# Who issues the stores of ScalarE's products: SyncE's queue or ScalarE's own

## The chip, the cores and the metric

The kernel runs on one core of a Trainium2 chip. The metric is the device time of one execution in microseconds (us). Below, the engines carry the names of the profile: PE is TensorE, with PEld its weight loads; DVE is VectorE, ACT is ScalarE, POOL is GpSimd, and SP is SyncE. Each engine works through its own list of instructions in order, and semaphores tie the lists together. A DMA is an instruction on the list of the engine that issues it; the bytes are then moved by 16 DMA engines beside the others. A trailing q, as in SPq or ACTq, means the engine's sequencer, which issues and waits.

## The reference

Two layers over a batch of 8 images of 384 channels and 32 x 32 pixels, all in float32. Cut to what matters:

```python
# layer 0, for each image: L = 1024 pixels as a sequence, forward and reversed
xn = rmsnorm(x)
u, z = split(xn @ in_proj)
u = silu(causal_conv1d(u) + b)
dt, B, C = split(u @ x_proj)                   # 24 + 16 + 16 columns
delta = softplus(dt @ dt_proj + dt_b)
h[t] = exp(delta * A) * h[t-1] + (delta * u) * B     # 16 states per channel
y = (sum_n h * C + u * D) * silu(z)
g = (y_forward + y_reversed) @ out_proj * scale_mod
x = x + res_scale * (g + sigmoid(dwconv3x3(xn)) * xn)
# layer 1
t = x + attention(layernorm(x))                # 6 heads of 64, causal, 1024 tokens
out = t + gelu(layernorm(t) @ kron(a, b).T) @ kron(c, d).T
```

## The kernel before

**An order planned ahead.** The whole program, 8 images through both layers, is first written as a list of operations, each with an engine, a cost, the values it reads and writes, and a wished-for time `at`. `Plan.run` (line 170) then plays the engines and one DMA pipe with these costs and fixes one order for everything. DMAs stand in that plan as operations of "SP" with a cost of 0.6 us. The loop at lines 1451 to 1461 emits the instructions in the planned order; each engine gets its own in that order.

**Stages of one image.** `project` makes u before the convolution, and `gates` makes z, both through `into` (line 707): PE multiplies, ACT copies each half out of PSUM (line 725), and for u the tile `ut` is stored to the DRAM array `urd` (line 727). `gates` then takes silu of the three tiles `zt` on ACT (line 740) and stores each in two halves to `uzd` through `blocks` (line 648, with `which` 1 for z and 0 for u). `prepare` loads `ct<-urd`, convolves, takes silu on ACT, and calls `products` (line 851), which makes B, C and dt in a tile `xd`; rows of B and C are stored to `bcd` (line 865). `deltas` sums the u of both directions on POOL (tile `us`, stored by `blocks` with `which` 0) and calls `delta` (line 868), which makes delta (`de`, stored to `ded` from POOL's result) and delta times u on POOL. The latter is split into three bf16 parts: ACT casts a part (line 905), two DMAs store its halves to `dusd` (line 907), POOL subtracts the part from the remainder (line 913), and so on. The tiles `part` share two buffers.

**The scan.** `scans` and `group` run the recurrence in 96 steps an image, on tiles `dA` of 128 rows (16 states by 8 channels) and 1024 time steps: a DMA loads delta (`dA<-ded`, 512 KB, 12 buffers), ACT takes exp (line 994), PE spreads the parts of delta u (`du<-dusd`) into PSUM tiles `b`, DVE multiplies by B (line 1009) and scans (line 1017), POOL multiplies by C (line 1020), PE sums over the states into `y`. `local`, `finish`, `attention`, `mix` and `forward` are the rest; while one image is scanned, the stages before the scan of the next images and those behind the scan of the same image run between its steps.

**What orders the DMAs.** All 1998 DMAs are issued by SP. The framework that turns the list into a program gives each DMA one of eight completion semaphores (DMAHW0 to DMAHW7) in turn, and each DMA first waits until the one that had this semaphore before, eight DMAs earlier in the program, has landed. So at most eight are on their way at a time. Buffers in SBUF and arrays in DRAM add waits of their own.

Of the kernel before, what the change touches and what calls it, by code (L numbers as in the profile page):

```python
# [17 lines left out]
P = 128  # L18
B, C, H, W = 8, 384, 32, 32
L = H * W  # L20
CT = C // P
# [3 lines left out]
NS = 16  # L25
# [15 lines left out]
KI, KO = 32, 12  # L41
# [63 lines left out]
class Plan:  # L105
# [13 lines left out]
    def op(self, engine, cost, fn, reads=(), writes=(), at=None, table=None, nbytes=0, holds=()):  # L119


        o = Op()
        o.engine, o.cost, o.fn, o.table, o.nbytes = engine, cost, fn, table, nbytes
        o.at = self.at if at is None else at
        o.placed = o.urgent = at is not None
        o.vals, o.allocs, o.users, o.ready, o.done = [], [], [], 0.0, None
        deps = set()

        def meets(a, b):
            return a is None or b is None or a == b  # L130

        for v in reads:
            v, part = v if isinstance(v, tuple) else (v, None)
            deps.update(w for w, q in v.writes if meets(part, q))
            v.reads.append((o, part))
            o.vals.append(v)
        for v in writes:
            v, part = v if isinstance(v, tuple) else (v, None)
            deps.update(w for w, q in v.writes if meets(part, q))
            deps.update(r for r, q in v.reads if meets(part, q))  # L140
            if part is None:
                v.writes, v.reads = [], []
            if v.kind is not None and v.left == 0 and v not in o.allocs:
                o.allocs.append(v)
            v.writes.append((o, part))
            o.vals.append(v)
        for v in holds:
            if v.left == 0 and v not in o.allocs:
                o.allocs.append(v)
            o.vals.append(v)  # L150
        deps.discard(o)
        o.vals = list(dict.fromkeys(o.vals))

        o.after, slot_of = [], set()
        for v in o.vals:
            v.left += 1
            if v in o.allocs:
                v.first = o
            elif v.first is not None and v.first not in deps:
                slot_of.add(v.first)  # L160
        for d in slot_of:
            d.after.append(o)
        o.waits = len(deps) + len(slot_of)
        for d in deps:
            d.users.append(o)
        o.index = len(self.ops)
        self.ops.append(o)
        return o
# [119 lines left out]
def conv_attn_hybrid_kernel(  # L288
# [20 lines left out]
    nc = tc.nc  # L309
# [28 lines left out]
    def half(hf):  # L338
        return slice(hf * HALF, (hf + 1) * HALF)
# [4 lines left out]
    def grid(t):  # L344
        return t.rearrange("p (r w) -> p r w", w=W)
# [63 lines left out]
    plan = Plan({k: n for k, (n, _) in kinds.items()})  # L409
    op = plan.op  # L410

    def dma(dst, src, reads, writes, nbytes, **kw):

        op("SP", 0.6, lambda: nc.sync.dma_start(dst(), src()), reads, writes, nbytes=nbytes, **kw)

    def tl(name, shape=(P, L), dtype=F32):
        return Val("t", list(shape), name, dtype)

    def bank(name):
        return Val("psm", [P, HALF], name)  # L420

    def accumulate(terms, p, cost, holds=(), **kw):

        for i, (args, reads) in enumerate(terms):
            first, last = i == 0, i == len(terms) - 1

            def term(args=args, first=first, last=last):
                mm(*args(), first, last)

            op("PE", cost, term, reads, [p], holds=holds if first else (), **kw)  # L430
# [39 lines left out]
    def arrays(shape, name, n, dtype=F32):  # L470
        return [array(shape, f"{name}_{i}", dtype) for i in range(n)]
# [10 lines left out]
    bcd = [arrays([2 * NS, L], f"bcd{d}", 2) for d in range(2)]  # L482
# [165 lines left out]
    def blocks(i, which, m, t, part):  # L648

        for a in range(2):  # L650
            dma(
                lambda a=a: uzd[i][2 * m + a].t[which].rearrange("(h p) t -> p h t", p=HC),
                lambda a=a: t.t[a * HC : (a + 1) * HC, :], [t], [(uzd[i][2 * m + a], part)], HC * L * 4,
            )

    def in_weights(b, w):
# [50 lines left out]
    def into(b, w, xp, win):  # L707

        s = b % 2
        ts = []  # L710
        for m in range(CT):
            t = tl(f"{'uz'[w]}t_{b}_{m}")
            for hf in range(NH):
                p = bank(f"pi_{b}_{w}_{m}_{hf}")

                accumulate(
                    [
                        (
                            lambda p=p, m=m, hf=hf, c=c: (grid(p.t), win.t[:, c, chans(m)], inside(xp[c].t, hf)),
                            [(xp[c], hf), win],  # L720
                        )
                        for c in range(CT)
                    ], p, pe(HALF), [t],
                )
                op("ACT", act(HALF), lambda p=p, t=t, hf=hf: nc.scalar.copy(t.t[:, half(hf)], p.t), [p], [(t, hf)])
            if w == 0:
                dma(
                    lambda m=m: urd[s].t[chans(m), TAPS - 1 : TAPS - 1 + L], lambda t=t: t.t, [t], [(urd[s], m)],
                    P * L * 4,
                )  # L730
            ts.append(t)
        return ts
# [118 lines left out]
    def products(b, d, us, wc):  # L851

        s = b % 2
        xd = tl(f"xd_{b}_{d}")
        for hf in range(NH):
            p = bank(f"px_{b}_{d}_{hf}")

            accumulate(
                [
                    (lambda p=p, hf=hf, c=c: (p.t, wc.t[:, c, 0:P], us[d][c].t[:, half(hf)]), [us[d][c], wc])  # L860
                    for c in range(CT)
                ], p, pe(HALF), [xd],
            )
            op("ACT", act(HALF), lambda p=p, hf=hf: nc.scalar.copy(xd.t[:, half(hf)], p.t), [p], [(xd, hf)])
        dma(lambda: bcd[d][s].t, lambda: xd.t[CT * KI : P, :], [xd], [bcd[d][s]], 2 * NS * L * 4)
        return xd

    def delta(b, d, c, du, xd):

        s = b % 2  # L870
        n = f"{b}_{d}_{c}"


        e, de, ln, w = (tl(f"{q}_{n}") for q in ("e", "de", "ln", "w"))
        ps = [bank(f"pd_{n}_{hf}") for hf in range(NH)]

        def both():
            for hf in range(NH):
                r = slice((c + hf) % CT * KI, (c + hf) % CT * KI + RANK)
                mm(ps[hf].t, w_dt[hf].t[r, :], xd.t[r, half(hf)])  # L880

        op("PE", pair(HALF), both, [xd] + [(w, c) for w in w_dt], ps, holds=[e, de])
        for hf in range(NH):

            def split(p=ps[hf], hf=hf):
                nc.scalar.activation(e.t[:, half(hf)], p.t, AF.Abs, bias=col("dt_b", c))
                nc.scalar.activation(de.t[:, half(hf)], p.t, AF.Relu, bias=col("dt_b", c))  # L887

            op("ACT", 2 * act(HALF) + 0.1, split, [ps[hf]], [(e, hf), (de, hf)])

        def logs():
            nc.scalar.activation(e.t, e.t, AF.Exp, scale=-1.0)
            nc.scalar.activation(w.t, e.t, AF.Identity, bias=ones[:, 0:1])
            nc.scalar.activation(ln.t, w.t, AF.Ln)
            nc.scalar.activation(w.t, w.t, AF.Identity, bias=minus)

        op("ACT", 4 * act(L) + 0.2, logs, [], [e, ln, w], table=EXP)
        op("POOL", pool(L), lambda: nc.gpsimd.tensor_sub(w.t, e.t, w.t), [e], [w])
        op("POOL", pool(L), lambda: nc.gpsimd.tensor_add(de.t, de.t, ln.t), [ln], [de])
        op("POOL", pool(L), lambda: nc.gpsimd.tensor_add(de.t, de.t, w.t), [w], [de])  # L900
        dma(lambda: ded[d][s].t[chans(c)], lambda: de.t, [de], [(ded[d][s], c)], P * L * 4)
        op("POOL", pool(L), lambda: nc.gpsimd.tensor_mul(du.t, de.t, du.t), [de], [du])
        for k in range(3):
            part = Val("t2", [P, L], f"part_{n}_{k}", BF16)
            op("ACT", act(L), lambda part=part: nc.scalar.copy(part.t, du.t), [du], [part])  # L905
            for hf in range(NH):
                dma(
                    lambda k=k, hf=hf: dusd[d][s].t[c * RG : (c + 1) * RG, hf, k],
                    lambda part=part, hf=hf: part.t[:, half(hf)], [part], [(dusd[d][s], (c, k, hf))], P * HALF * 2,
                )  # L910
            if k < 2:
                op(
                    "POOL", pool(L), lambda part=part: nc.gpsimd.tensor_sub(du.t, du.t, part.t), [part], [du]  # L913
                )
# [609 lines left out]
```

## Time and profile before

| | |
|---|---|
| three runs | 3931.32, 3935.32 and 3963.04 us, median 3935.32 |
| the profiled execution | 3941.6 us |
| its span, from the first to the last instruction | 3939.9 us |
| busy share of the span | PE 90%, DVE 85%, POOL 76%, ACT 72% |
| DMA packets' time on the one data queue, as a share of 16 engines' span | 77.5% |
| mean granted TensorE clock | 0.929 |

Busy shares are means over stages with different limits. The page also has each engine's share in 40 slices of the span, the chain of work that ended last, and the costliest groups of instructions by line; answers of the trace give waits, single lines, stretches and the order of time.

### The profile page before, as it was taken

The page shows a single profiled execution, that of the slowest core. Times are in us where ns is not written, and L with a number is a line of the kernel's source. Part 1 is how long each engine was busy: PE and PEld are TensorE (multiplying, and loading weights), DVE is VectorE, ACT ScalarE, POOL GpSimd, SP SyncE. Part 2 cuts the span into 40 slices and gives each one's busy share as a digit, 9 for nine tenths or more (in the row PEclk, how much of TensorE's full clock was granted, in tenths as well). Part 3 has the DMA queues.
Part 4 walks back from the last instruction along what each step waited for, and adds up shares of the span by engine and source line. Part 5 has one row for each costly group of instructions (what it writes and reads, how often), then busy time and mean ns, then how long its engine had stood idle before and what let it go on. Part 6 is the DMA issues. An engine that isn't in the chain of part 4 may idle for free.

```text
span 3939.9 us, 54075 instructions
## 1 busy us (share of the span) xinstructions
PE 3545.6 (90%) x17970; PEld 1386.8 (35%) x17970; DVE 3362.0 (85%) x4403; ACT 2821.3 (72%) x4465; POOL 2999.4 (76%) x2370
## 2 busy tenths in 40 slices
PE   7477768899999999899999999999999988999998
PEld 3011112443244432443234432443234431443363
DVE  1489998899988999899998999799898999999522
ACT  4665645887788867786788868887778866676464
POOL 2888986997699956998589966998579966676231
PEclk9587778999999999899999999999998998999999
DMA  8889899689966998689966998779976897678101
GB/s 266 238 253 281 250 262 245 179 235 269 273 201 201 259 264 244 183 241 256 276 207 187 255 271 249 199 230 248 257 231 170 219 253 189 168 197 227 44 9 37
DMA packets 301999, 858.92 MB, mean 218 GB/s; under 512 B 38312, under 2 KB 91576, under 8 KB 301720
## 3 DMA queue, kind: packets, MB, share of 16 engines
q1 hardware_dynamic: 301720, 855.47, 77.5%
q8 instruction: 143, 2.34, 0.3%
q14 instruction: 136, 1.11, 0.1%
HBM read 696.44 MB, written 160.68 MB: 218 GB/s over the span
## 4 chain that ended last, share of the span: by engine, by line
DVE 33%; PE 25%; DMA 15%; POOL 12%; issue 7%; ACT 7%; SPq 1%; POOLq 0%; DVEq 0%; ACTq 0%
DVE dA L1017 20%; DVE b L1009 7%; DMA dA<-ded 5%; POOL dA L1020 5%; PE t L1254 3%; PE pc L331 3%; PE y L331 2%; PE s L331 2%; PE pq L331 2%; POOL p L1244 2%; PE b L331 2%; DVE mx L1190 2%; DMA dusd<-part 1%; DMA yg<-ygd 1%; PE pi L331 1%
## 5 line engine op out<-in xcount | busy, mean ns | idle before, releaser
L1020 POOL TENSOR_TENSOR dA<-dA,bc 128x1024 f32<-128x1024 f32 x768 | 1808.7, 2366 | 579.5 <-DVE dA L1017 405.8
L1017 DVE TENSOR_TENSOR_SCAN dA<-dA,b 128x512 f32<-128x512 f32 x1536 | 1906.1, 1242 | 36.4 <-ACT dA L994 18.1
L1009 DVE TENSOR_TENSOR b<-b,bc 128x512 f32<-128x512 f32 x1536 | 986.3, 683 | 166.7 <-PE b L331 160.6
L994 ACT ACTIVATE dA<-dA,nA 128x1024 f32<-128x1024 f32 x768 | 864.3, 1146 | 311.6 <-DMA dA<-ded 270.6
L331 PE MATMUL b<-du,dup 32*128 32x512 bf16 x1536 | 412.9, 407 | 218.8 <-DVE dA L1017 160.4
L331 PE MATMUL y<-dA,sel 128*32 128x512 f32 x3072 | 485.3, 651 | 8.3 <-POOL dA L1020 6.3
L1190 DVE TENSOR_REDUCE mx<-s 128x1 f32<-128x512 f32 (+3 forms) x576 | 287.3, 546 | 170.2 <-PE s L331 166.3
L1197 ACT ACTIVATE p<-s,mx 128x512 f32<-128x512 f32 (+3 forms) x576 | 330.9, 580 | 115.6 <-DVE mx L1190 114.7
L1244 POOL TENSOR_SCALAR p<-p,den 128x512 f32<-128x512 f32 (+3 forms) x576 | 328.7, 590 | 83.4 <-DVE den L1236 66.8
L1254 PE MATMUL t<-ident,p 128*128 128x128 f32 x1728 | 286.2, 303 | 51.0 <-ACT p L1197 19.2
L331 PE MATMUL s<-k,q 64*128 64x512 f32 (+3 forms) x1152 | 302.7, 552 | 20.3 <-ACT p L1197 18.4
L1261 ACT COPY pT<-t 128x512 f32<-128x512 f32 (+1 forms) x480 | 245.5, 547 | 96.1 <-PE t L1254 87.9
L331 PE MATMUL pi<-xp,win 128*128 128x512 f32 x576 | 300.3, 640 | 13.9 <-ACT de L887 6.3
L1460 ACT ACT_TABLE_LOAD x224 | 287.4, 1283 | 4.7 <-PEq L1513 0.8
L331 PEld LDWEIGHTS <-dup 32*128 32x128 bf16 x1536 | 76.6, 92 | 593.9 <-issue 572.3
L1254 PEld LDWEIGHTS t<-ident,p 128*128 128x128 f32 x1728 | 208.3, 152 | 204.7 <-POOL p L1244 123.9
L331 PE MATMUL pc<-pT,v 128*64 128x128 f32 x3456 | 251.0, 291 | 6.2 <-ACT pT L1261 5.4
L331 PEld LDWEIGHTS pc<-pT,v 128*64 128x64 f32 x3456 | 199.6, 144 | 113.9 <-ACT pT L1261 52.9
L913 POOL TENSOR_TENSOR u<-u,part 128x1024 f32<-128x1024 f32 x96 | 205.2, 2138 | 26.0 <-ACT part L905 25.9
L905 ACT CAST part<-u 128x1024 bf16<-128x1024 f32 x144 | 150.5, 1045 | 88.5 <-DMA dusd<-part 45.2
L331 PEld LDWEIGHTS y<-dA,sel 128*32 128x32 f32 x3072 | 74.4, 111 | 296.1 <-POOL dA L1020 137.4
L331 PEld LDWEIGHTS s<-k,q 64*128 64x128 f32 x1152 | 110.5, 191 | 176.2 <-ACT p L1197 72.8
(183 smaller groups left out, 4741.8 us busy)
## 6 DMA issues: line engine op xcount, KB each, us to landing
dA<-ded SPq DMA_DIRECT2D x768, 512.0 KB
ct<-urd SPq DMA_DIRECT2D x96, 513.5 KB
du<-dusd SPq DMA_DIRECT2D x96, 512.0 KB
xs<-xpd SPq DMA_DIRECT2D x96, 432.8 KB
dusd<-part SPq DMA_DIRECT2D x288, 128.0 KB
ded<-de SPq DMA_DIRECT2D x48, 512.0 KB
uz<-uzd SPq DMA_DIRECT2D x48, 512.0 KB
bc<-bcd SPq DMA_DIRECT2D x32, 512.0 KB
```

The source lines that it names most:

```text
L331: return nc.tensor.matmul(out_, lhsT=lhsT, rhs=rhs, start=first, stop=last)
L913: "POOL", pool(L), lambda part=part: nc.gpsimd.tensor_sub(du.t, du.t, part.t), [part], [du]
L994: "ACT", act(L) + 0.1, lambda: nc.scalar.activation(dA.t, dA.t, AF.Exp, scale=nA.t[:, g : g + 1]),
L1009: "DVE", dve(HALF), lambda v=v, hf=hf: nc.vector.tensor_mul(v.t, v.t, bc.t[:, 0, half(hf)]), [(bc, 0)], [v],
L1017: nc.vector.tensor_tensor_scan(t, t, v.t[:, rev], h, ALU.mult, ALU.add)
L1020: op("POOL", pool(L), lambda: nc.gpsimd.tensor_mul(dA.t, dA.t, bc.t[:, 1]), [(bc, 1)], [dA], at=at - PRODUCTS)
L1190: lambda sc=sc, g=g, w=k1 - k0, hh=hh: nc.vector.tensor_reduce(mx.t[:, g, hh : hh + 1], sc[hh].t[:, 0:w], AX.X, ALU.max, negate=True), [sc ...
L1197: nc.scalar.activation(ps[g].t[:, hh, 0 : k1 - k0], sc[hh].t[:, 0 : k1 - k0], AF.Exp, bias=mx.t[:, g, hh : hh + 1], accum_out=den.t[:, g, ...
L1244: nc.gpsimd.tensor_scalar(t, t, den.t[:, g, hh : hh + 1], 1.0, ALU.mult, ALU.mult)
L1254: nc.tensor.transpose(t.t[:, o + j * P : o + (j + 1) * P], ps[g].t[:, hh, j * P : (j + 1) * P], ident)
L1261: nc.scalar.copy(pT[g].t[:, hs[0] : hs[-1] + 1, 0:w], t.t[:, 0 : len(hs) * w].rearrange("p (h w) -> p h w", w=w))
L1460: nc.scalar.preload_act_table_set(table)
```

## The change

The helper `dma` gets an argument `queue`, which is SP's by default. At four places it is now ACT's: the stores `dusd<-part` (288 of them), `uzd<-zt` (48), `urd<-ut` (24) and `bcd<-xd` (16), 376 in all. The stores of u for the gate (`uzd<-us`), which POOL makes, stay with SP, and so do all loads. The plan still counts these stores as operations of SP, so the order is what it was: each of the 376 stands on ACT's list at the place that the planned order gives it among ACT's instructions.

```diff
-    def dma(dst, src, reads, writes, nbytes, **kw):
-
-        op("SP", 0.6, lambda: nc.sync.dma_start(dst(), src()), reads, writes, nbytes=nbytes, **kw)
+    def dma(dst, src, reads, writes, nbytes, queue=nc.sync, **kw):
+
+
+        op("SP", 0.6, lambda: queue.dma_start(dst(), src()), reads, writes, nbytes=nbytes, **kw)
...
             dma(
                 lambda a=a: uzd[i][2 * m + a].t[which].rearrange("(h p) t -> p h t", p=HC),
                 lambda a=a: t.t[a * HC : (a + 1) * HC, :], [t], [(uzd[i][2 * m + a], part)], HC * L * 4,
+                queue=nc.scalar if which else nc.sync,
             )
...
                     lambda m=m: urd[s].t[chans(m), TAPS - 1 : TAPS - 1 + L], lambda t=t: t.t, [t], [(urd[s], m)],
-                    P * L * 4,
+                    P * L * 4, queue=nc.scalar,
                 )
...
-        dma(lambda: bcd[d][s].t, lambda: xd.t[CT * KI : P, :], [xd], [bcd[d][s]], 2 * NS * L * 4)
+        dma(lambda: bcd[d][s].t, lambda: xd.t[CT * KI : P, :], [xd], [bcd[d][s]], 2 * NS * L * 4, queue=nc.scalar)
...
                     lambda part=part, hf=hf: part.t[:, half(hf)], [part], [(dusd[d][s], (c, k, hf))], P * HALF * 2,
+                    queue=nc.scalar,
                 )
```

The eight completion semaphores are still handed out in turn over all 1998 DMAs, whichever engine issues them.

## The prediction

> **What bounds the kernel now.** I read the page first (busy shares, slices, chain), then the stretches of 450 us, which is about one image, then the waits of SP and of the other engines, then the one line that issues DMAs.
>
> ```profile
> PE 3545.6 (90%) x17970; PEld 1386.8 (35%) x17970; DVE 3362.0 (85%) x4403; ACT 2821.3 (72%) x4465; POOL 2999.4 (76%) x2370
> DMA  8889899689966998689966998779976897678101
> DVE 33%; PE 25%; DMA 15%; POOL 12%; issue 7%; ACT 7%; SPq 1%; POOLq 0%; DVEq 0%; ACTq 0%
> ```
>
> The chain jumps between all engines: none alone is the bound. The stretches say it by image (us, then busy us of PE, PEld, DVE, ACT, POOL, then clock and DMA share):
>
> ```profile
> 1000.00:1450.00 450.00, 428.09 (x2256) 171.08 (x2256) 420.50 (x548) 356.01 (x563) 376.25 (x294) 0.97 0.84 238
> 1450.00:1900.00 450.00, 422.65 (x2219) 170.54 (x2218) 411.77 (x537) 352.02 (x557) 369.28 (x289) 0.96 0.84 234
> 1900.00:2350.00 450.00, 430.78 (x2259) 170.84 (x2258) 419.15 (x545) 354.69 (x562) 373.54 (x292) 0.96 0.82 238
> ```
>
> PE has some 23 of 450 us left, DVE 33, POOL 77, ACT 96. PE and DVE set the pace, in a fixed order in which each often takes what ACT has just made. Does SP hold anyone up? Its own waits (us, times, longest):
>
> ```profile
> SPq L414 <- PE y L331: 728.2, 252, 9.5
> SPq L414 <- DMA dA<-ded: 253.9, 203, 2.9
> SPq L414 <- ACT part L905: 153.7, 60, 6.8
> ```
>
> The first is SP waiting for a dA buffer to come free: there SP is ahead of the others. The second is the rotation of eight semaphores. Only the third belongs to the stores that are moved. Who waits for DMAs:
>
> ```profile
> ACT dA L994 <- DMA dA<-ded: 270.6, 161, 9.1
> ACT part L905 <- DMA dusd<-part: 45.2, 23, 6.7
> PE b L331 <- DMA du<-dusd: 32.3, 2, 29.6
> ```
>
> Almost all of it is ACT, while DVE waits only 18.1 us in all for the exp of dA. So SP is not the bound after the first image; late loads cost ACT time, and ACT is ahead for the scan.
>
> **Step 1: what leaves SP.** The line that issues DMAs (ns: least, median, most):
>
> ```profile
> L414 SPq DMA_DIRECT2D dusd<-part x288: 502/558/4787, 104.7 to 3130.3; - x144
> L414 SPq DMA_DIRECT2D uzd<-zt x48: 574/600/2217, 247.1 to 2850.0; - x48
> L414 SPq DMA_DIRECT2D urd<-ut x24: 319/534/2898, 36.7 to 2659.3; - x24
> ```
>
> 288 x 0.558 + 48 x 0.600 + 24 x 0.534 + 16 bcd stores at some 0.46 = 210 us of issuing leave SP, and with them its waits for ACT at the head of its list: 153.7 for part, 19.7 for xd, 6.0 for ut, 3.6 for zt, 183 us together. SP's other 1622 DMAs keep their order. This is worth what the loads behind gain by coming earlier. Bounds: 0 (SP only waits longer for buffers) and 109 us. The latter is what the chain spends on the moved stores in flight (69 us, 47 of them in the first 600 us) and on SP's sequencer (40 us, 33 of them there).
>
> Here a rule of the Trainium skill stands against the change. "DMA: Bandwidth & Descriptors", section "Issuing engines are not separate DMA queues": the transfers of all issuing engines run on the same 16 engines, so a second issuer saves issue time and nothing else. By the rule the gain is 210 us on an engine that is not the bound, near 0. By the trace there is more: a part store lands 6.7 us after its issue (median of the landings) but 2.8 at the least, since it stands behind loads of 512 KB in SP's queue, and ACT waits 45.2 us for that, its two part buffers being still read. The same page, "Queues, rings and completion order", gives SP and ACT rings of their own, served in turn by packets. No run here shows a second queue yet. I take half of the 45.2 plus a fifth of the 69 us: a gain of **35 us**; the bandwidth is the rule's, since the DMA share is 0.90 to 1.00 from 300 to 600 us and the bytes are the same.
>
> **Step 2: the issuing on ACT.** The same 210 us come onto ACT, which had 2821 busy. No row shows ACT issuing. The skill's "Perfetto Trace Analysis", section on the HWDGE DMA instruction, says that the issuing sequencer itself sits through the semaphore wait, a lock on the descriptor generator and the generation before it takes its next instruction. By that rule alone, all 210 us hold ACT. The trace shows a cover: ACT's 802 semaphore instructions start at the median 0.36 us *before* the end of the ACTIVATE ahead of them (one at 692.75 us, when the ACTIVATE of line 336 began at 692.73 and ran 0.58), so the sequencer is up to one instruction ahead, and an issue can run beside the instruction ahead of it. In the changed program's order 232 of the 376 stand behind another ACT instruction than their producer, 122 directly behind another store, and 22 directly behind the cast or copy that they store. The 232 I cost at nothing (an exp of dA lasts 1.15 us, a copy 0.59); if that cover fails they are 130 us. The rest, 144 x 0.57, is 83 us of ACT. How much of ACT's lateness reaches the path? Pairing semaphores in the trace, three in ten of the ACT results that others wait for are taken within 0.74 us of being ready and half within 1.6. A pair of stores makes ACT about 0.6 to 1.1 us late, so I take half: **+40 us**. Ends: 0 and 140 (nothing hidden, two thirds through).
>
> **Step 3: waits that ACT takes on.** This is the added wait. Each store waits for the DMA eight before it in the program, and in 267 of 376 cases that is one of SP's. Behind it on ACT stand exps, PSUM evictions (lines 725, 1261) and softmax exps, for which PE and DVE wait. I laid the waits of the changed order on the landing times of this trace and let ACT run on from each store: 82 us of waiting, 31 of it between 400 and 600 us, 51 at the zt stores. Such a place (SP's list, then ACT's):
>
> ```profile
> 1483.11 5.08 SPq L414 DMA_DIRECT2D uzd<-zt  x4
> ...
> 1484.16 2.07 ACT L1369 ACTIVATE g<-ph 128x512 f32<-128x512 f32 x4
> 1488.40 1.09 ACT L1369 ACTIVATE g<-ph 128x512 f32<-128x512 f32 x2 [2.17 <-PE ph L331]
> ```
>
> Three of these four stores now stand together on ACT behind the gelu that ends at 1485.2; the last needs a dA load that SP issued at 1481 and that landed at 1491.6, so ACT would stand 6 us and the gelu at 1488.4 come 3 us late. In the other direction, the stores land earlier than in this trace and SP issues earlier. I take half of 82: **+40 us**. Ends: 0, and 131 us (all through, plus the later waits that each slip causes).
>
> **The sum.** -35 + 40 + 40 = +45 us on the profiled execution's 3941.6 us, so 3986.6. That execution lies 6.3 us above the median of the runs, hence **3980 us**, 1.1% above it. A measurement of this kernel (its three runs are 0.8% apart) tells about 1% from no change.
>
> **Rivals.**
> - *SP's freedom pays (faster).* The price is at the head and at each stall of ACT for a dA load. If the DMA engines, busy 0.80 to 0.88 in the first 300 us and 0.83 later, are filled because SP no longer stands 183 us at unfinished stores, the gain of step 1 comes near its 109 us and a third of ACT's 270.6 us of waits for loads goes too. With ACT's costs all hidden the time is some 3941.6 - 110 + 30 - 6 = 3855; with half of it, 3890. It decides from the point where gains exceed the 80 us of steps 2 and 3. For it: the chain's 15% on DMA. Against: SP's largest wait is for free buffers, and PE and DVE are over 91% busy in the middle.
> - *They cancel (within 1%).* Step 3 shrinks because stores land in 3 us rather than 6.7, and PE takes ACT's lateness from its 23 us of slack an image: 3935 + 0 to 20, say 3945.
> - *A convoy (slower by more).* ACT waits for a load that SP may issue only when a dA buffer is free, which needs DVE, POOL and PE, which wait for ACT's evictions. Then both ends of steps 2 and 3 apply: +140 + 131 - 35 = +236, 4170; a half of it, 4050. For it: 267 waits across the two lists; against: in steady images only some 10 of 47 stores meet a late predecessor.
> - *No change of order at all* is excluded: the order of PE, DVE and POOL is the same and ACT's list only gains 376 DMAs, while SP's loses them.
>
> **Chances.** My forecast and its neighbourhood (slower, up to 4050) 0.37, the convoy 0.10, cancelling 0.28, SP's freedom 0.25. Slower by over 1% 0.47, within 1% 0.28, faster by over 1% 0.25. The 8-in-10 range goes from half of the first rival to a little over half of the convoy: 3880 to 4070. As cases of both signs hold much of it, the forecast's own range is 3950 to 4040.
>
> **What the profile after would show.** Step 1: two data queues on the page; SP's wait for ACT part gone and its waits for PE y longer by about as much; ACT part waiting for dusd stores well under 45 us. Step 2: DMA rows on ACT near 0.56 us and its idle time an image down by some 10 to 25 us. Step 3: waits at ACT's sequencer for dA loads, some 5 to 10 us at each group of zt stores; PE waiting more for ACT in evictions. Wrong if PE and DVE finish an image in clearly under 450 us (the first rival), or if ACT's stores take several us each in the median (the convoy).

## The result and the profile after

| | before | after |
|---|---|---|
| median of the runs | 3935.78 us (4 runs, 3931.32 to 3963.04) | 3999.69 us (4 runs, 3998.09 to 4024.85) |
| ratio, with its 95% interval | | 1.0159 [1.0122, 1.0195] |
| profiled execution, its span | 3941.6, 3939.9 us | 4001.22, 3999.2 us |
| mean granted TensorE clock | 0.929 | 0.916 |

The change costs 64 us between the medians and 63 us by the ratio. All ratios in this document are of fast runs, which leaves out one slow run, the one of 4015.44 us of `act_extra`.

Of the page after: busy times, the DMA share in slices, the two data queues and the chain.

```profile
PE 3563.0 (89%) x17970; PEld 1396.3 (35%) x17970; DVE 3364.0 (84%) x4403; ACT 2821.7 (71%) x4465; POOL 2997.2 (75%) x2370
DMA  7879889679966997679966898669976797678101
q1 hardware_dynamic: 252568, 790.45, 70.9%
q10 hardware_dynamic: 49152, 65.02, 4.8%
...
DVE 16%; PE 15%; DMA 6%; POOL 5%; issue 3%; ACT 3%; ACTq 0%; POOLq 0%; DVEq 0%; SPq 0%
```

A second data queue is there and carries the moved stores: 65 of 855 MB. No engine's work grew, PE's 17 us apart; the same work stands further apart. The shares of this chain sum to under half of the span, so I don't compare it with the one of before. The stretches of an image (us, then busy us of PE, PEld, DVE, ACT, POOL, then clock, DMA share and GB/s):

```profile
1000.00:1450.00 450.00, 419.97 (x2186) 169.85 (x2182) 403.78 (x525) 344.69 (x548) 365.87 (x288) 0.94 0.82 228
1450.00:1900.00 450.00, 423.44 (x2205) 170.08 (x2204) 408.48 (x531) 348.82 (x554) 368.23 (x289) 0.94 0.82 231
1900.00:2350.00 450.00, 417.14 (x2184) 168.31 (x2185) 405.44 (x528) 351.47 (x557) 364.46 (x288) 0.94 0.82 229
```

DVE did 420.50, 411.77 and 419.15 us of work in these stretches and now does 403.78, 408.48 and 405.44. It loses some 3 to 17 us in each. SP's waits (us, times, longest):

```profile
SPq L415 <- PE y L331: 1077.4, 285, 18.5
...
SPq L415 <- DMA dA<-ded: 244.1, 159, 5.4
...
SPq L415 <- DMA dusd<-part: 76.5, 28, 7.4
```

SP is free of its waits for the ACT products that it stored before, which were 153.7 us for `part` alone (2.2 are left). It spends the time waiting for a dA buffer: 1077 us in place of 728. It also waits 76.5 us for stores of `part` that were eight DMAs before its own (16.0 before). The waits of ACT:

```profile
ACT dA L997 <- DMA dA<-ded: 230.3, 132, 11.6
...
ACT part L907 <- DMA dusd<-part: 47.3, 19, 8.5
...
ACT g L1372 <- DMA uzd<-zt: 20.8, 3, 7.8
ACT g L1372 <- DMA dA<-ded: 15.0, 2, 7.6
```

ACT's wait for its part buffers, which was to shrink from 45.2 us, is 47.3. New are gelus (`g`) that wait for a store of z or for a dA load, which none of them reads: they wait because a store stands ahead of them on ACT's list. The waits of PE and DVE that go with it, after, and the one of DVE before:

```profile
PE pz L331 <- ACT g L1372: 27.5, 5, 6.9
...
DVE b L1012 <- PE b L331: 198.4, 66, 102.6
```

```profile
DVE b L1009 <- PE b L331: 160.6, 52, 95.2
```

PE had no such wait for a gelu before; it now has five of them. DVE, whose own work is the same, waits 38 us longer for `b`. The stores themselves, on their new engine (ns: least, median, most):

```profile
L415 ACTq DMA_DIRECT2D dusd<-part x288: 511/527/1742, 107.5 to 3196.1; - x144
L415 ACTq DMA_DIRECT2D uzd<-zt x48: 582/588/1244, 247.7 to 2908.8; - x48
L415 ACTq DMA_DIRECT2D urd<-ut x24: 321/344/593, 30.2 to 2726.0; - x24
```

An issue on ACT takes no longer than it took on SP (558, 600 and 534 ns in the median). A place where it hurts, in order of time:

```profile
1517.28 9.26 SPq L415 DMA_DIRECT2D dA<-ded  x4
...
1523.11 0.60 ACT L1372 ACTIVATE g<-ph 128x512 f32<-128x512 f32 x1
1523.35 0.58 ACTq L415 DMA_DIRECT2D uzd<-zt  x1
...
1523.61 0.59 ACT L1372 ACTIVATE g<-ph 128x512 f32<-128x512 f32 x1
...
1525.33 4.54 ACTq L415 DMA_DIRECT2D uzd<-zt  x2
...
1529.92 2.06 ACT L1372 ACTIVATE g<-ph 128x512 f32<-128x512 f32 x4 [5.72 <-DMA uzd<-zt]
...
1530.57 1.92 PE L331 MATMUL pz<-g,w_p 128*32 128x512 f32 x4 [3.24 <-ACT g L1372]
...
1533.07 1.30 DVE L1012 TENSOR_TENSOR b<-b,bc 128x512 f32<-128x512 f32 x2 [4.73 <-PE b L331]
```

The store at 1523.35 is issued while a gelu runs and costs nothing: the next gelu starts at 1523.61. The pair at 1525.33 is the last of its z group. Its second store takes the completion semaphore of a dA load that SP issued at 1518.20 and that landed at 1529.27, so ACT stands 3.4 us of the 4.54. The gelu behind it comes 5.7 us late (in the trace before, this gelu and its three neighbours ran in a row from 1484.16), PE's next product waits 3.24 us for that gelu, the matmuls for `b` stand behind the product on PE, and DVE waits 4.73 us. One load of SP has held up three engines, through a store that has nothing to do with it.

SP did not issue that load late for want of a buffer. Pairing the semaphores, it issued the load 0.1 us after the DMA that had the semaphore before had landed (1518.13). The load was long on its way: 11.1 us from issue to landing, where the median of the dA loads in this trace is 8.6. The last z store of each of the images 3 to 7 (counted from 0) tells the same: a dA load issued at most 0.4 us after its semaphore had come free, 11.1 to 12.0 us on its way, and ACT standing 3.4 to 5.9 us.

The standing of ACT at a store is the time for which its sequencer has the store next and waits for the DMA of eight before to land. Paired so, the trace after has 115 us at 53 stores, of them 61.9 at 25 z stores and 47.6 at 23 part stores. Of the z stores' share 27.8 lie in the first 650 us. An ACT instruction that still runs covers a part: counted from its end, some 90 us are left, 55 at z stores and 33 at part stores.

### The profile page after: what moved, and what is told of

The parts are those of the page before. It is cut to its first block, busy times and chain, and to the rows that moved or that the text cites. A ratio compares the mean times of both kernels' runs of the same rounds, so it can differ in the third digit from the quotient of the medians.

```text
span 3999.2 us, 53926 instructions
## 1 busy us (share of the span) xinstructions
PE 3563.0 (89%) x17970; PEld 1396.3 (35%) x17970; DVE 3364.0 (84%) x4403; ACT 2821.7 (71%) x4465; POOL 2997.2 (75%) x2370
## 5 line engine op out<-in xcount | busy, mean ns | idle before, releaser
L1012 DVE TENSOR_TENSOR b<-b,bc 128x512 f32<-128x512 f32 x1536 | 986.9, 683 | 199.2 <-PE b L331 198.4
L331 PE MATMUL s<-k,q 64*128 64x512 f32 (+3 forms) x1152 | 312.5, 560 | 30.1 <-ACT p L1200 17.1
L907 ACT CAST part<-u 128x1024 bf16<-128x1024 f32 x144 | 150.2, 1044 | 83.8 <-DMA dusd<-part 47.3
L1372 ACT ACTIVATE g<-ph 128x512 f32<-128x512 f32 x192 | 103.6, 596 | 119.4 <-PE ph L331 79.2
```

The source lines that it names most:

```text
L331: return nc.tensor.matmul(out_, lhsT=lhsT, rhs=rhs, start=first, stop=last)
L1012: "DVE", dve(HALF), lambda v=v, hf=hf: nc.vector.tensor_mul(v.t, v.t, bc.t[:, 0, half(hf)]), [(bc, 0)], [v],
```

## The experiments

Each ran beside the kernel before. Losses in us are those of the ratio: 0.1% is 3.9 us, so 1.0159 is 63 us, and a bracket of us gives the interval. Behind every change of queue each engine still issues its DMAs in the same order, but which DMA is eight before which is not quite the same: by the traces 431 of the 1998 have another completion semaphore in the changed kernel than before, and 80 in `zt_only`.

### Only z's stores, and only the parts'

`zt_only`: the 48 stores of z from ACT, the 328 others from SP.

```diff
-                    P * L * 4, queue=nc.scalar,
+                    P * L * 4, queue=nc.sync,
...
-        dma(lambda: bcd[d][s].t, ..., 2 * NS * L * 4, queue=nc.scalar)
+        dma(lambda: bcd[d][s].t, ..., 2 * NS * L * 4, queue=nc.sync)
...
-                    queue=nc.scalar,
+                    queue=nc.sync,
```

> Of the 376 moved stores only the 48 of silu(z) are issued by ScalarE; the other 328 stay with SyncE as before. Theory A (the loss of the whole change, some 64 us, is ScalarE standing at stores whose DMA of eight before has not landed, mainly a load of SyncE at the second store of a z pair): these 48 had 61.9 us of such waiting of 115 in the trace of the changed kernel and carry most of the steps in its loss, so some 40 of the 64 us are here: about 3976 us. Theory B (each issue on ScalarE's busy list costs a share of its 0.57 us: 64/376 = 0.17 us a store): 48 x 0.17 = 8 us, about 3944 us. Theory C (the loss comes from SyncE, which, freed of its waits for ScalarE, sends loads and other stores earlier into full queues): these are 48 of 376 stores, the bulk of the freed waiting is elsewhere, about 3944 us.

Measured: 3967.17 us, ratio 1.0081 [1.0052, 1.0109], 32 us (20 to 43). 48 stores cost four times what an equal price per store gives. ACT stood 58.0 us at them. Theory A had said 40, which lies within the interval; the 8 us of theories B and C do not.

`dusd_only`: the 288 stores of the parts from ACT, the rest from SP (the edit is of the same kind).

> Only the 288 stores of the parts of delta u are issued by ScalarE; silu(z), u, B and C stay with SyncE. Theory A (waits for the DMA of eight before at ScalarE): 47.6 of the 115 us of waiting lay at these stores, but 47.6 us of ScalarE waiting for their landing was there before too; steps of +5 near 2050 us and a share of the first 650 us: some 15 us, about 3952 us. Theory B (a price per issue): 288 x 0.17 = 49 us, about 3985 us. Theory C (SyncE freed): most of the freed waiting is at these stores, about 3980 us.

Measured: 3960.32 us, 1.0061 [1.0040, 1.0082], 24 us. Theory A's 15 us lie just under the interval (16 to 32 us), and the equal price's 49 and theory C's 44 above it. So six times as many stores cost no more than the 48.

### The z stores later on ACT's list

`zt_late`: the changed kernel, each z store (`behind`) written after the `BEHIND` = 8 ACT operations that follow, or earlier where its data or its buffer is needed.

```diff
     for o in order:
...
+        if o in behind:
+            held.append((n_act + BEHIND, o))
+            continue
         o.fn()
+        n_act += o.engine == "ACT"
+        while held and held[0][0] <= n_act:
+            held.pop(0)[1].fn()
```

> The changed kernel, with each store of silu(z) written on ScalarE's list behind the eight ScalarE operations that follow (or earlier, where its data is read or its slot is reused), so that the DMA of eight before has had 5 to 8 us more to land. Same number of issues, same owner. Theory A: the waiting at these stores (61.9 us) goes, with most of the steps at the z groups: about 3965 us, if the stores written in between do not take over the wait. Theory B (price per issue): nothing changes, 4000 us. Theory C (SyncE freed): nothing changes, 4000 us.

Measured: 3964.85 us, 1.0073 [1.0047, 1.0100], against 1.0159 for the changed kernel: 34 us come back, near theory A's 35, with as many issues by the same owners. ACT's standing at the z stores fell from 61.9 to 15.0 us, and at the parts it stayed (44.5). The kept trace is of one of its two fastest runs (3948.81 us). The same group, of image 4, in this kernel:

```profile
1493.43 0.65 ACTq L416 DMA_DIRECT2D uzd<-zt  x1
1493.70 0.59 ACT L1375 ACTIVATE g<-ph 128x512 f32<-128x512 f32 x1
1494.11 0.82 ACTq L416 DMA_DIRECT2D uzd<-zt  x1
...
1497.61 0.58 ACTq L416 DMA_DIRECT2D uzd<-zt  x1
1497.70 2.17 ACT L1000 ACTIVATE dA<-dA,nA 128x1024 f32<-128x1024 f32 x2
1499.37 0.58 ACTq L416 DMA_DIRECT2D uzd<-zt  x1
1499.78 1.14 ACT L1000 ACTIVATE dA<-dA,nA 128x1024 f32<-128x1024 f32 x1
1503.02 1.28 ACTq L416 DMA_DIRECT2D uzd<-zt  x2
```

The last pair takes 1.28 us where it took 4.54. 34 us for 47 us less of standing is 0.7 us per us. Eight operations later also puts the stores at other places among the work and gives most of them another DMA of eight before (29 of the 48 a dA load, 9 in the changed kernel), so this alone doesn't say that the standing is the cause; together with `zt_stall` below it does.

### What the plain time of issuing costs

`act_extra`: all stores from SP; a copy in ACT's list at each of the 376 places.

```diff
+        def issue():
+            nc.sync.dma_start(dst(), src())
+            if queue is nc.scalar:
+                nc.scalar.copy(idle.rearrange("p (k n) -> p k n", n=P), ones.unsqueeze(1).to_broadcast([P, 4, P]))
```

> The kernel before, every store with SyncE, with a ScalarE copy of 128x512 (some 0.58 us, no wait, to a buffer that nothing reads) at each of the 376 places where the changed kernel issues a store from ScalarE. It has the time of the issue without its wait, its queue or SyncE's relief, and rather more than the issue since it occupies the engine's datapath. Theory B (issue time is what costs): the loss of the change or more, 4000 us and above. Theory A: the plain time of issuing is mostly slack of ScalarE (71 to 76% busy), some 0.03 to 0.08 us of each on the path: 3945 to 3965 us. Theory C: the same as A.

Measured: 3975.59 us, 1.0075 [1.0049, 1.0101], 30 us (19 to 40). The group of the copies (busy us, mean ns, idle before):

```profile
L419 ACT CAST idle<-ones 128x512 bf16<-128x512 f32 x376 | 231.2, 615 | 3.9
```

231 us more on ACT make the end 30 us later: one part in eight. An issue of a part store takes 527 ns, less than a copy, and in the trace of the changed kernel 278 of the 376 begin while an ACT instruction runs, as above at 1523.35. So I take the 30 us as an upper bound for step 2.

### What a stop of several us at the z stores costs

`zt_stall`: all stores from SP; at the 24 places of the last store of a z tile, four long copies on ACT.

```diff
+            nc.sync.dma_start(dst(), src())
+            if stall:                          # z, second half
+                for k in range(4):
+                    nc.scalar.copy(idle.rearrange("p (k n) -> p k n", n=P), ones.unsqueeze(1).to_broadcast([P, L // P, P]))
```

> All stores with SyncE as before. At the 24 places where ScalarE would issue the last store of a silu(z) tile, it does four copies of 128x1024 instead (4 x 1.05 = 4.2 us, to a buffer that nothing reads), 101 us in all. Theory A (a stop of some us at this place reaches the end by half or more, unlike short issues spread over the list, of which a seventh did): +50 us or more, about 3990 us. Rival B (time on ScalarE costs a seventh wherever it lies, and what cost in the z stores was their queue): +14 us, about 3953 us.

Measured: 4020.24 us, 1.0195 [1.0168, 1.0221], 77 us (66 to 87).

```profile
L420 ACT CAST idle<-ones 128x1024 bf16<-128x1024 f32 x96 | 100.3, 1045 | 2.5
```

77 of 100 us reach the end, three quarters, with no store on ACT. ACT's time is worth 0.13 us per us when it is spread in short pieces over the list, and 0.77 in pieces of 4 us between silu(z) and the gelus. That is enough for the z stores: 0.77 x 58 us of standing is 45 us, somewhat over what `zt_only` measured (20 to 43); of the 58 some 49 are not covered by a running ACT instruction, and 0.77 x 49 is 38.

The path is the same one. PE's wait for gelus before `pz` is 27.5 us in the changed kernel, 26.6 in `zt_only` and 33.2 in `zt_stall`; the traces of the kernel before, of `zt_late` and of `no_zt` list none, and that of `act_extra` 1.0. DVE's wait for `b` goes along: 198.4, 190.7 and 218.1 us against 160.6, 156.7, 164.9 and 165.2.

### Everything but z

`no_zt`: the changed kernel with the 48 z stores back on SP.

```diff
-                queue=nc.scalar if which else nc.sync,
+                queue=nc.sync,
```

> The changed kernel with the 48 stores of silu(z) given back to SyncE; the other 328 (parts of delta u, u, B and C) stay with ScalarE. Theory A (two costs that add: some 0.08 us for each issue, as 376 extra copies on ScalarE cost 30 us, and half of ScalarE's waits at the z stores, as z stores alone cost 28 to 32 us): what is left is 328 x 0.08 = 26 us, about 3965 us. A rival D (the loss is an interaction: it takes both groups on ScalarE, as each delays the other's predecessors): well above the sum's part, 3975 us or more, or well below, 3950. Theory C (SyncE freed is what costs): nearly all of SyncE's relief is still there, so nearly all of the loss, about 3990 us.

Measured: 3958.77 us, 1.0032 [1.0013, 1.0051], 13 us (5 to 20). This kernel has 328 of the 376 issues, most of SP's relief (its wait for a dA buffer is 1016 us) and 44 us of standing at part stores. Theory C, by which SP's relief costs, falls (3990). So does a price per issue of more than 0.06 us, and with it theory A's 26 us; rival D's lower figure, 3950 us or some 11 of loss, is the nearest. `zt_only` and `no_zt` together make 45 us, not the 63 of the whole. The 13 us are less than the 24 (16 to 32) of `dusd_only`, which moves 40 stores fewer; with those 24 the sum would be 56. So what these stores cost alone is known only as 5 to 32 us.

### The part buffers

`part3_b`: the kernel before, its order kept, the parts in three buffers in turn.

```diff
+                if v.kind == "t2":
+                    v.slot, parts = parts % 3, parts + 1
                 v.t = p.tile(v.shape, v.dtype, tag=f"{v.kind}_{v.slot}", name=v.name)
```

> The kernel before, stores with SyncE, the same order, but the parts of delta u go round three buffers instead of two. ScalarE's wait for a part's store to land (45 us) and most of SyncE's 16 us for it should go. The prediction's first step took half of such a wait as gain. If that holds: some 15 to 20 us less, about 3920 us. Rival (the wait lies in slack, as ScalarE waits for its dA loads next, 270 us): no change, 3939 us.

Measured: 3934.43 us, 0.9990 [0.9971, 1.0009]. The wait is gone, and no gain is seen; the interval leaves room for 11 us at most:

```profile
ACT dA L994 <- DMA dA<-ded: 270.8, 148, 8.9
...
ACT part L905 <- DMA dusd<-part: 2.2, 2, 1.6
```

Most or all of the 45.2 us were slack. ACT waits for its dA loads as before.

`part3_a`: the same three buffers in the changed kernel.

> The changed kernel, stores with ScalarE, the same order, the parts of delta u in three buffers instead of two. Theory A: the 47 us wait for the landing goes, but the stores' own wait for the DMA of eight before and the z stores' stay: some 10 us less than the changed kernel, about 3990 us. Rival (the loss of the change is mostly this buffer wait, since the stores land later from ScalarE's queue: 7.8 against 6.9 us): most of the loss goes, about 3955 us.

Measured: 4002.06 us, 1.0144 [1.0119, 1.0169]: no difference to the changed kernel that these intervals show. The wait for a buffer turned in part into the stores' wait for the DMA of eight before (68.2 us at part stores, 47.6 in the changed kernel).

### The whole once more, and a version without the table loads

`after_again`: the changed kernel once more, no edit.

> The changed kernel once more, beside the kernel before on the chip of this call, to narrow the size of the loss. If the two costs found add (z stores: 58 to 62 us of waiting, of which about three quarters reach the end as a stop at this place did, 45 us; the other 328 stores 13 us): 58 us, a ratio of 1.0147. If the z stores cost with the others on ScalarE what they cost alone (32 us): 45 us, a ratio of 1.0114. If the groups disturb each other: above 1.018.

Measured: 4015.64 us, 1.0184 [1.0160, 1.0207], 72 us (63 to 82). With 63 us in the first comparison, the two groups of stores together cost 18 to 27 us more than `zt_only` and `no_zt` add up to, or 7 to 16 more than `zt_only` and `dusd_only`. By the totals alone the sum of two costs, which I had put forward with `no_zt`, is doubtful but not refuted. The traces say more.

I took the start of each DVE instruction after less its start before (DVE's list is the same in all these kernels) and the median over stretches, in us:

```
from us   after  after_again  zt_only  no_zt  zt_stall  part3_b  z_steady  z_head
   400      9.4      12.2       3.9     3.2     14.5      1.0       4.2     11.2
   600     15.8      19.0       3.4     0.5     20.7     -2.4       0.1     18.6
   900     18.3      23.5       5.8     3.1     20.6     -2.3       1.9     22.1
  1100     34.3      39.7      19.4     7.4     39.9     -3.2      13.6     33.8
  1500     42.3      47.8      26.3     9.1     53.9     -5.5      22.4     34.6
  2300     54.7      52.6      26.1    13.9     59.7     -7.7      38.1     43.3
  2500     67.2      63.7      32.9    26.9     73.4     -7.9      52.0     46.8
  3700     59.4      69.2      22.0    10.2     78.6     -8.9      38.2     40.1
```

By 650 us the changed kernel is 16 to 19 us late in its two traces, while each group alone is 0.5 to 3.4 us late (`dusd_only` is 3.8 ahead). There the groups meet: z stores of images 1 and 2 and part stores of image 1 stand among each other between 490 and 575 us, and ACT's standing at z stores in the first 650 us is 28 us against 17 with z alone. The two kernels on the right were made to test that.

### The z stores of the head and of the rest

`z_steady`: the changed kernel with the 18 z stores of images 0 to 2 back on SP; `z_head`: with the 30 of images 3 to 7 back on SP.

```diff
-                queue=nc.scalar if which else nc.sync,
+                queue=nc.scalar if act else nc.sync,
...
-            blocks(b % 3, 1, m, zs[m], "z")
+            blocks(b % 3, 1, m, zs[m], "z", b > 2)      # z_head: b <= 2
```

> The changed kernel, but the z stores of the first three images (18 stores, in the first 600 us) are given back to SyncE; those of the other five (30) stay with ScalarE, and so do all other moved stores. The z stores alone cost 32 us, all others alone 13 us, together 64 to 75 us: some 20 to 28 us come only together. Theory E (they come together in the head, where both kinds of store wait in the same 60 us, 58 us of waiting there against 17 and 24 us alone): without the head's z stores what is left is 13 us and the steady z stores' waits, 34 to 42 us at three quarters: 26 to 32 us; 3982 us, a ratio of 1.011. Rival F (they disturb each other all along): 1.014 or more.

> The counterpart: the z stores of the first three images (18) with ScalarE, those of the other five (30) back with SyncE, all other moved stores with ScalarE. Theory E: 13 us and the head's loss, 16 to 19 us by the first 600 us of the two traces of the changed kernel: 3971 us, a ratio of 1.008. Rival F: 13 us and the head's z stores by their share of waiting when alone (17 of 58 us of waiting, 9 of the 32 us): 3962 us, a ratio of 1.0055.

Measured: `z_steady` 3982.11 us, 1.0099 [1.0061, 1.0137], 39 us (24 to 54); `z_head` 3983.17 us, 1.0104 [1.0069, 1.0139], 41 us (27 to 55). Less the 13 us of `no_zt`, the z stores of the steady images cost 26 us and the 18 of the head 28, each to within some 16 us; with the 13 that makes 67, between the 63 and 72 of the whole. The first 650 us of before, after, `z_steady` and `z_head`, in this order (columns as above):

```profile
0.00:650.00 650.00, 460.28 (x1542) 119.04 (x1546) 479.51 (x597) 362.52 (x401) 484.67 (x268) 0.76 0.90 257
```

```profile
0.00:650.00 650.00, 446.40 (x1482) 117.57 (x1486) 465.06 (x580) 354.18 (x393) 473.09 (x263) 0.74 0.86 253
```

```profile
0.00:650.00 650.00, 456.66 (x1542) 119.09 (x1546) 480.33 (x597) 360.64 (x401) 484.48 (x268) 0.77 0.87 257
```

```profile
0.00:650.00 650.00, 445.48 (x1468) 117.61 (x1468) 461.90 (x577) 354.10 (x392) 471.70 (x262) 0.75 0.87 251
```

DVE finishes 597 instructions in the head before and with `z_steady`, 580 after and 577 with `z_head`. So 18 z stores make the head's whole loss, but only beside the part stores (`zt_only` finishes 594). Whether that is the crowding of stores or the other pairing of DMAs with semaphores, no run separates. Theory E stands in its place, the head; its size for `z_head` was 30 us and the run gave 41, both within the interval. Rival F's 1.0055 for `z_head` lies below the interval, its 1.014 for `z_steady` just above. By 650 us `z_head` is 18.6 us late, and then loses some 12 us more by 1100 us, where it has no z store on ACT. In its trace ACT waits 27.4 us for dA loads between 900 and 1100 us, where it waited 9.0 before; `dusd_only`, with part stores alone, waits 27.2 there and loses 12 us too. Why those loads come late stays open.

### Less ACT time at the z groups

If ACT's time there is worth three quarters, cutting it should gain. `swap`: the kernel before, with short runs of other work put behind the second of two runs of gelu (`MOST` is 4 operations).

```diff
     order = plan.run()
+    for (t0, _), (t1, mid), (t2, nxt) in ...:    # runs of ACT operations between two table loads
+        if t0 == t2 == GELU and len(mid) <= MOST and pull(mid, nxt):   # nxt ahead of mid, where nothing in it needs mid
+            ...
```

> The kernel before, stores with SyncE, with one change to ScalarE's order: where a short run of other work (up to 4 operations, mostly the exponentials of dA) stands between two runs of GELU and the second run does not depend on it, it is put behind the second run. Two loads of the function table (1.28 us each) go each time, 41 of 224 in all, 52 us of ScalarE's time, most of them in the stretch around the z tiles. If ScalarE's time there reaches the end at three quarters, as in the run with extra work: 0.76 x 52 = 40 us less, about 3900 us; less if the exponentials now come late for VectorE (each by one run of GELU, 1 to 4 us, and up to 41 times): no change or slower, 3940 to 3980 us.

Measured: 3953.97 us, 1.0031 [1.0015, 1.0048], 12 us slower. The loads of the table did go:

```profile
L1508 ACT ACT_TABLE_LOAD x183 | 234.8, 1283 | 4.0 <-PEq L1561 0.8
```

ACT does 53 us less and the end comes later. By 650 us this kernel is 7 us ahead (the same DVE instructions compared), and it loses 15 between 900 and 1500 us. So a stop costs three quarters there, but work taken away at the price of another product's lateness is not paid back at that rate. That later exponentials of dA eat it up was argued before the run, and the trace speaks against it: between 900 and 1500 us DVE waits 1.1 us for them, as before, but 12.1 us for PE's `b` where it waited 4.5. What holds PE there is open. No version that I ran beats the kernel before.

## Why the prediction was right, and where its steps were not

The forecast was 3980 us and slower; the result is 3999.69, 1.6% above before, within the range. Step 3's mechanism was right. That the sum came near, +45 us against 63 to 72 measured, is in part luck, as its terms were wrong on opposite sides.

- **Step 1, a gain of 35 us: none shows.** It took 22.6 us for half of ACT's 45.2 us wait, on the ground that a store on ACT's own queue would not stand behind SP's loads. The stores land no sooner: medians from issue to landing were 6.9 and 6.2 us for the two directions' part stores before, and 7.8 and 6.7 after; u's went from 7.6 to 8.5, z's from 7.2 to 7.0 (7.7 in the trace of `after_again`). And the wait was worth little anyway (`part3_b`, 0.9990). The rule that I set against the trace, the Trainium skill's "DMA: Bandwidth & Descriptors", section "Issuing engines are not separate DMA queues", was the better guide: transfers from ACT interleave with those from SP on the same engines, and only issue time is saved. SP's freed time went into its wait for dA buffers, 728 to 1077 us. I departed from the rule on the strength of a landing of 2.8 us at the least; the least landing is 2.8 us after the change too, and says nothing of the median. No run frees SP without loading ACT, so that the gain is just zero isn't shown; `no_zt` gives gains less costs of 328 stores, a loss of 5 to 20 us.
- **Step 2, a cost of 40 us: too large.** 376 real copies cost 30 us, and the 328 moved stores without z's, with their issuing and their waits, cost 13 after whatever step 1 gave. The cover is real: 278 of the 376 issues begin beside a running ACT instruction, and I had counted on 232. What I got wrong is the share that passes: I took a half from how soon others take ACT's results, and for short pieces the extra work shows one eighth.
- **Step 3, a cost of 40 us: too small.** Its mechanism and its place were right: waits for the DMA eight before, at the z groups, with SP's dA loads as the late ones. Its 82 us of standing measured 115, and the half that I let through is three quarters for a stop of 4 us at the z stores. The z stores make some 54 of the 67 us that the runs account for (26 and 28), and 34 us come back when they stand eight operations later.
- **What the sum had no term for:** the two kinds of store disturb each other. 58 us of ACT's standing in the head (28 at z, 30 at parts) cost 16 to 19 us there, where each kind alone left the kernel at most 3.4 us late.
- **The rivals.** *SP's freedom pays* fell on its own argument against: SP's largest wait was for free buffers and grew. (Its 3855 us also do not follow from its text: they add 30 us that it does not name and leave out the third of 270.6 us that it grants.) *They cancel* was close for the 328 stores (13 us), not for the 48. The *convoy* begins at the z groups, where one load holds up ACT, PE and DVE, but it does not feed on itself: the loss comes in steps and stays flat between them (16.8 us at 700 us, 18.3 at 900), and the load that ACT waits for was not held back by a full set of dA buffers.
- **What the profile was to show.** Two data queues, SP's wait for ACT gone and its wait for PE y longer, issues near 0.56 us on ACT, and waits of ACT for dA loads at the z stores: all there, the last with 2 to 7 us at a place. PE waits more for ACT, but for the gelus before `pz` (27.5 us) rather than for evictions. Part waits well under 45 us: wrong, and this was the sign that step 1 had failed. ACT's idle time down by 10 to 25 us an image: wrong, it is up by some 11 in the first stretch, as issuing is not counted as busy and a standing ACT is idle.

## What to carry to other kernels

A store put on a computing engine's list brings along every wait that the store has, and not only the one for its data: here the reuse of a completion semaphore tied ACT to loads of SP that have nothing to do with it. Ask for each moved DMA what it waits for besides its data and whether that can be late; writing the same stores eight operations later gave 34 of 63 us back. And price a wait by where it lies, not by its share of the busy time: the same microsecond of ACT was worth about 0, 0.13 and 0.77 at the part buffers, spread over the list, and ahead of the gelus.

## What the hardware showed that I had not expected

- A queue of its own did not make a store quicker: from ACT's queue, with 65 MB in all, the 288 part stores landed 7.1 us after their issue in the median (6.9 in `after_again`), and 6.7 from SP's queue with 855.
- ACT's sequencer issues a DMA while an ACTIVATE runs: 0.58 us at 1523.35 between two gelus that follow each other at 1523.11 and 1523.61. In return, a DMA that must wait holds back the ACTIVATE behind it, though that one reads nothing of it: ACT is idle for 5.72 us before the gelu at 1529.92.
- With eight semaphores in turn, a slow landing is handed on: at the z groups of images 3 to 7 a dA load was issued when the DMA eight before it had landed, took 11.1 to 12.0 us itself (8.6 in the median of all), and held up an ACT store of eight later for 3.4 to 5.9 us.
- The granted TensorE clock went down with the time: 0.922 to 0.932 in runs of the kernel before, 0.913 to 0.919 in those of the changed one, 0.915 to 0.919 in those of `zt_stall`. In the 84 runs of the kernel before that stand beside the experiments it goes along with the time too (correlation -0.65). PE's busy time grew by 17 of the 64 us. Whether a part of the loss is PE running slower after stops, or the lower clock is only their mark, these runs don't tell; `zt_stall` lost more than the changed kernel at much the same clock.
